# An LSTM step whose unit groups share PSUM columns through zero-padded stationary h, with the RNN beside it in bf16 parts

## The chip, the cores and the metric

The kernel runs on one core of a Trainium2 chip. The metric is the device time of one execution in microseconds, from the first to the last instruction of that core. The kernel before the change takes 4678.84 us (median of 3 runs, 4676.4 to 4680.62).

## The reference

The input is x of 4 x 1024 x 512 (batch B = 4, T = 1024 time steps, width D = 512) and one conditioning vector of 512 per batch row. Four residual layers follow one another, all float32:

```
x = x + rnn(x)        # h = tanh(x_t @ Wx + b + h @ Wh), 1024 steps in a row, Wh 512 x 512
x = x + ssm(x)        # 4-tap conv, projections, state = decay*state + dt*B_t*u_t, output projection
x = x + lstm(x)       # A = x_t @ Wx + b + h @ Wh, Wh 512 x 2048
                      # c = sigmoid(f)*c + sigmoid(i)*tanh(g);  h = sigmoid(o)*tanh(c), 1024 steps in a row
x = x + adapt(x)      # x @ (base + low-rank matrix made from the conditioning vector)
```

The RNN and the LSTM are the recurrences: step t needs the h of step t - 1, and the h of only four batch rows at a time. Everything else can be done for many time steps at once.

## The kernel before, in words

Features lie on the partitions: a vector of 512 is 128 partitions x KC = 4 columns. The time axis is cut into 32 chunks of TC = 32 steps. The main loop (`do_pass`, L815) makes one LSTM step per turn. In the same turn it makes one RNN step, which runs LEAD = 56 steps ahead, and the jobs that a table gives for this place in the chunk: input projections of the RNN (`project0`) and of the LSTM (`input_mm`, L334), the state-space layer (`ssm_jobs`), the last layer (`adapt_mm`, L754). A job stands at "pe" (TensorE, before the RNN's matmuls), "gap" or "end" (VectorE and ScalarE). The order of the instructions on every engine is the order in which this loop writes them; nothing reorders it. Steps before the first LSTM step (the first 56 RNN steps) also load and prepare the weights; these loads are paced by RNN steps (`paced`, L688).

One LSTM step works on h of 128 partitions x 4 columns x 4 batch rows. To get float32 precision from bf16 matmuls, h is split in NP = 3 parts, each the upper 16 bits of what is left (`split`, L208, on VectorE), and Wh in three bf16 parts (`wh2`). In `lstm_mm` (L375 to L388) the 12 columns of a matmul's stationary side are the three parts of h for four batch rows; the moving side is one part of Wh. TensorE is used as four column tiles of 32, one per j, which compute units 128 j to 128 j + 127 and write PSUM partitions 32 j on. The step is cut in two halves of the units, mh = 0 (called A) and mh = 1 (called Bh), with an accumulator `acc2` of 128 x 256 each: 4 gates x 64 units. Per half there are 4 k x 3 parts x 4 tiles = 48 matmuls of 256 columns; kh says which half of h is multiplied, so that A's h of the step before is used first.

Then each half goes through the same chain (class `Half`): VectorE transposes 32 x 32 blocks of `acc2` (L403, gates i, f, g as 128 x 192, gate o as 128 x 64), so that features lie on partitions again; adds the three partial sums and the input part, which ScalarE has copied beside them (L391, L409); ScalarE takes tanh of the gates (L416); VectorE makes products and the cell (L429, L434); ScalarE takes tanh of the cell (L439); VectorE makes h (L442) and splits it twice (L208). A's and Bh's chains are interleaved by hand in `do_pass`.

One RNN step is `rnn_mm` (L349): 4 k x 4 tiles of float32 matmuls with 4 stationary and 128 moving columns, for each of which the profile has two matmul records. Then one transpose of 128 x 128 (L368), one add of the input part (L369), and tanh on ScalarE (L372), which writes h0.

TensorE's order in a turn is: A's matmuls with A's h, a few of Bh's, A's with Bh's h, the rest of Bh's, the "pe" job, the RNN's. GpSimd has nearly nothing to do after the start, where it issues small loads, makes an identity matrix (`make_identity`, L212) and clears buffers.

Of the kernel before, what the change touches and what calls it, by code (L numbers as in the profile page):

```python
# [14 lines left out]
P = 128  # L15
B, T, D = 4, 1024, 512
KC = D // P
TC = 32
# [13 lines left out]
EPS = 1e-5  # L32
XBUFS = 3
# [6 lines left out]
def cond_resid_kernel(ctx: ExitStack, tc: tile.TileContext, a: dict, out: bass.AP):  # L40
# [66 lines left out]
    h2 = [state.tile([P, KC, TC, NP, B], F32, name=f"h2{i}", tag=f"h2{i}") for i in range(2)]  # L107
# [5 lines left out]
    tt2 = [turns(2, f"tt2{m}", [P, 4, 2, B + CT]) for m in range(2)]  # L113
# [3 lines left out]
    tt0 = turns(1, "tt0", [P, KC, CT])  # L117
# [16 lines left out]
    wh0 = load_rows(const, "wh0", a["Wh0"], D, nc.sync)  # L134
# [81 lines left out]
    nc.vector.tensor_scalar(h2[1][:, :, TC - 1, 0, :], condT, 2.0, None, ALU.mult)  # L216
    for n in range(1, NP):
        split(h2[1][:, :, TC - 1], n)
# [6 lines left out]
    acc2 = [psum.tile([P, 2 * P], F32, name=f"acc2{i}", tag=f"acc2{i}") for i in range(2)]  # L225
# [63 lines left out]
    def split_wh2(k, g):  # L289
# [3 lines left out]
        left = xw2[g % 2][:, 2 + g // 2].rearrange("p c t b -> p (c t b)")  # L293
        return (
            lambda: nc.scalar.activation(part[0], upper(w), AF.Copy, scale=scale),
            lambda: nc.vector.scalar_tensor_tensor(left, w, scale, part[0], ALU.mult, ALU.subtract),
            lambda: nc.scalar.copy(part[1], upper(left)),
# [51 lines left out]
    def rnn_mm(c, t):  # L349
        h = h0[c % 2] if t else h0[(c - 1) % 2]  # L350
        for k in range(KC):
            for j in range(4):
                nc.tensor.matmul(  # L353
                    acc0[CT * j : CT * j + B, :],
                    h[:, k, (t - 1) % TC, :], wh0[:, k, j * P : (j + 1) * P],
                    start=(k == 0), stop=(k == KC - 1),
                )
# [7 lines left out]

    def rnn_pre(c, t):
        tt, pre = tt0[0], pre0[t % 2]
        nc.vector.transpose(tt.rearrange("p c b -> p (c b)"), acc0)  # L368
        nc.vector.tensor_add(pre, xw0[c % 2][:, :, t, :], tt[:, :, :B])  # L369

    def rnn_h(c, t):
        nc.scalar.activation(h0[c % 2][:, :, t, :], pre0[t % 2], AF.Tanh)  # L372
# [20 lines left out]
    class Half:  # L393
# [24 lines left out]
        def transpose_o(self):  # L418
            self.transpose(3, 4)
# [559 lines left out]
```

## Time and profile before

| | |
|---|---|
| median of the runs | 4678.84 us |
| span of the profiled execution | 4689.2 us |
| TensorE matmuls, busy | 4552.4 us, 97%, 146,816 instructions |
| TensorE weight loads, busy | 3581.8 us, 146,816 instructions |
| VectorE, busy | 3956.1 us, 84% |
| ScalarE, busy | 1876.6 us, 40% |
| GpSimd, busy | 48.7 us, 1% |
| first LSTM matmul | at 151.3 us |
| one LSTM step | 4.38 us in nearly all steps |

Times are of one profiled execution, in microseconds unless ns is said. In a line of the groups stand the source line, the engine, the operation, output and inputs by name, shapes (partitions x elements), the count, then the busy time and the mean ns of one, and after the bar the idle time of the engine just before such instructions with what ended it. PE is TensorE's matmul, PEld its weight load, DVE VectorE, ACT ScalarE, POOL GpSimd. "issue" is time in which an engine waited for nothing that the profile shows. A line of the DMA queues has packets, MB, and the packets' time as a share of 16 DMA engines over the window. A chain line has start, length and what ran.

### The profile page before, as it was taken

How to read it: one execution, taken by the hardware profiler on the slowest of the kernel's cores; microseconds unless marked ns; L12 is line 12 of the kernel's file. 1: busy time of each engine (PE TensorE's matmuls, PEld its weight loads, DVE VectorE, ACT ScalarE, POOL GpSimd, SP SyncE). 2: the span in 40 equal slices, each digit the busy share in tenths (PEclk: the TensorE clock that was granted, in tenths of full speed). 3: DMA queues.
4: the chain of work that ended last, by engine and by line, in shares of the span. 5: the costliest groups of instructions: out<-in, count | busy, mean ns of one | idle time of the engine just before them, and what ended most of it. 6: DMA issues, size and time to landing. Idle time of an engine off the chain costs nothing.

```text
span 4689.2 us, 326423 instructions
## 1 busy us (share of the span) xinstructions
PE 4552.4 (97%) x146816; PEld 3581.8 (76%) x146816; DVE 3956.1 (84%) x22102; ACT 1876.6 (40%) x9693; POOL 48.7 (1%) x91
## 2 busy tenths in 40 slices
PE   7999999999999999999999999999999999999986
PEld 5777777777877777777777877777777777777754
DVE  4688888888888888888888888888888888888876
ACT  3334444444444444443444444444443444444333
POOL 3000000000000000000000000000000000000000
PEclk9999999999999999999999999999999999999999
DMA  6300000000000000000000000000000000000000
GB/s 155 102 24 7 9 7 9 9 7 9 9 7 9 9 7 9 9 7 9 9 7 9 9 7 9 9 7 9 9 7 9 9 7 9 9 5 7 6 6 8
DMA packets 40234, 67.77 MB, mean 14 GB/s; under 512 B 8864, under 2 KB 26016, under 8 KB 38320
## 3 DMA queue, kind: packets, MB, share of 16 engines
q1 hardware_dynamic: 35792, 46.55, 3.7%
q8 instruction: 1147, 18.79, 1.7%
q14 instruction: 255, 2.09, 0.1%
q0 software_dynamic: 1696, 0.19, 0.0%
q10 hardware_dynamic: 1344, 0.14, 0.0%
HBM read 38.34 MB, written 8.39 MB: 10 GB/s over the span
## 4 chain that ended last, share of the span: by engine, by line
PE 91%; DVE 7%; issue 1%; DMA 0%; POOL 0%; ACT 0%; SPq 0%; DVEq 0%; POOLq 0%
PE acc L384 55%; PE acc L353 18%; PE proj L334 9%; PE pb L308 3%; DVE tt L403 3%; DVE gc L409 2%; PE proj L308 2%; PE ada L754 2%; DVE prod L429 1%; PE ssm_out L308 1%; DVE h L208 1%; PE idle L308 0%; PE pp L616 0%; DVE h L442 0%; DVE tt L368 0%
## 5 line engine op out<-in xcount | busy, mean ns | idle before, releaser
L384 PE MATMUL acc<-wh,h 128*12 128x256 bf16 x98304 | 2908.8, 273 | 96.6 <-DVE h L208 91.0
L384 PEld LDWEIGHTS <-h 128*12 128x12 bf16 x98304 | 2316.3, 87 | 549.0 <-DVE h L208 194.0
L403 DVE STREAM_TRANSPOSE tt<-acc 128x192 f32<-128x192 f32 (+1 forms) x4096 | 1236.6, 310 | 291.0 <-PE acc L384 267.8
L416 ACT ACTIVATE gc<-gc 128x24 f32<-128x24 f32 (+1 forms) x4096 | 854.4, 216 | 1388.5 <-DVE gc L409 1382.9
L353 PEld LDWEIGHTS acc<-wh,h 128*4 128x4 f32 x32768 | 811.6, 87 | 498.9 <-issue 204.2
L353 PE MATMUL acc<-wh,h 128*4 128x128 f32 x32768 | 1089.4, 273 | 12.4 <-ACT h L372 6.6
L409 DVE TENSOR_REDUCE gc<-tt 128x24 f32<-128x96 f32 (+1 forms) x4096 | 1038.9, 255 | 70.5
L208 DVE TENSOR_TENSOR h<-h 128x8 f32<-128x8 f32 (+1 forms) x4098 | 673.2, 164 | 69.9
L372 ACT ACTIVATE h<-pre 128x16 f32<-128x16 f32 x1024 | 221.6, 216 | 1130.9 <-DVE pre L369 1130.9
L439 ACT ACTIVATE th<-gc 128x8 f32<-128x8 f32 x2048 | 427.9, 209 | 261.9 <-DVE gc L434 225.4
L334 PE MATMUL proj<-wx,x 128*32 128x512 f32 x4096 | 530.5, 592 | 0.3 <-issue 0.3
L442 DVE SCALAR_TENSOR_TENSOR h<-gc,th 128x8 f32<-128x8 f32 x2048 | 328.8, 161 | 143.6 <-ACT th L439 133.9
L368 DVE STREAM_TRANSPOSE tt<-acc 128x128 f32<-128x128 f32 x1024 | 316.3, 309 | 68.9 <-PE acc L353 68.8
L429 DVE SCALAR_TENSOR_TENSOR prod<-gc 128x16 f32<-128x16 f32 x2048 | 348.7, 170 | 12.7
L391 ACT COPY tt<-xw 128x32 f32<-128x32 f32 x2048 | 327.9, 207 | 0.0
L434 DVE SCALAR_TENSOR_TENSOR gc<-prod 128x8 f32<-128x8 f32 x2048 | 298.6, 146 | 0.0
L369 DVE TENSOR_TENSOR pre<-xw,tt 128x16 f32<-128x16 f32 x1024 | 180.2, 176 | 37.6
L308 PE MATMUL proj<-xin,wx 128*32 128x128 f32 x4096 | 138.6, 277 | 17.5 <-DMA wh<-in_Wh_dram 11.8
L754 PE MATMUL ada<-layer,x 128*32 128x512 f32 (+1 forms) x1056 | 134.8, 587 | 2.7 <-DVE x L747 2.6
L308 PE MATMUL pb<-x,wp 128*32 128x128 f32 x4096 | 134.7, 273 | 1.0 <-issue 0.6
L308 PEld LDWEIGHTS proj<-xin,wx 128*32 128x32 f32 x4096 | 117.0, 112 | 22.1 <-DMA wh<-in_Wh_dram 11.8
L334 PEld LDWEIGHTS proj<-wx,x 128*32 128x32 f32 x4096 | 119.6, 110 | 5.5 <-issue 0.5
(125 smaller groups left out, 1159.1 us busy)
## 6 DMA issues: line engine op xcount, KB each, us to landing
layer<-in_w2T_dram SPq DMA_DIRECT2D x32, 512.0 KB, 4.6
xin<-in_xT_dram SPq DMA_DIRECT2D x128, 64.0 KB, 2.7
out_dram<-x SPq DMA_DIRECT2D x124, 64.0 KB, 2.1
wx<-in_Wx_dram SPq DMA_DIRECT2D x20, 256.0 KB, 5.1
layer<-in_Wh_dram SPq DMA_DIRECT2D x16, 256.0 KB, 6.0
wh<-in_Wh_dram SPq DMA_DIRECT2D x4, 256.0 KB, 8.3
layer<-in_w_dram SPq DMA_DIRECT2D x4, 256.0 KB, 4.5
layer<-in_base_dram SPq DMA_DIRECT2D x4, 256.0 KB, 8.1
```

What stands on the lines that cost most here:

```text
L208: nc.vector.tensor_tensor(h[:, :, n], h[:, :, n - 1], upper(h[:, :, n - 1]), ALU.subtract)
L308: nc.tensor.matmul(dst[CT * j : CT * (j + 1)], columns(j), x, start=first, stop=final)
L334: nc.tensor.matmul(ps[CT * j : CT * (j + 1), :], tok, w[:, j], start=(k == 0), stop=(k == KC - 1))
L353: nc.tensor.matmul(acc0[CT * j : CT * j + B, :], h[:, k, (t - 1) % TC, :], wh0[:, k, j * P : (j + 1) * P], start=(k == 0), stop=(k == KC - 1),
L384: nc.tensor.matmul(acc2[mh][CT * j : CT * j + NP * B, :], upper(h[:, k, (t - 1) % TC].rearrange("p s b -> p (s b)")), w[:, :, n0 : n0 + 2 ...
L391: nc.scalar.copy(tt2[m][t % 2][:, :, :, :B], xw2[c % 2][:, :, 2 * m : 2 * m + 2, t, :])
L403: nc.vector.transpose(self.tt[:, g0:g1, :, B:].rearrange("p g c b -> p (g c) b"), acc2[self.m][:, 2 * CT * g0 : 2 * CT * g1],)
L409: nc.vector.tensor_reduce(self.gc[:, to : to + g1 - g0].rearrange("p g c b -> p (g c) b"), self.tt[:, g0:g1, :, : (1 + NP) * B].rearrange( ...
L416: nc.scalar.activation(self.gc[:, g0:g1], self.gc[:, g0:g1], AF.Tanh, scale=0.5)
L429: nc.vector.scalar_tensor_tensor(self.prod, self.gc[:, 0:2], 1.0, self.gc[:, 2:4], ALU.add, ALU.mult)
L439: nc.scalar.activation(self.th, self.c, AF.Tanh, scale=0.5)
L442: nc.vector.scalar_tensor_tensor(self.out[:, :, 0], self.gc[:, 4], 1.0, self.th, ALU.add, ALU.mult)
```

## The change

In `lstm_mm` a half's 64 units per tile are cut in two groups of 32, s = 0 and s = 1, which share the same 128 columns of `acc2` (4 gates x 32 units). h's parts are kept as pairs (zeros, h) in a buffer `ring`; a matmul whose stationary columns begin at the zeros has h in the odd blocks of four rows, one that begins four columns later has h in the even blocks. Stationary columns are 24 for s = 1 and 20 for s = 0. So a half takes 96 matmuls of 128 columns and its accumulator is 128 x 128. Each half has one transpose for all gates; the sums of i, f, g and of o stay apart.

`ring` has two halves of KEEP = 4 time steps; in every fourth step GpSimd copies h out of it to `h2` (`keep_h2`) and to `h0` (`keep_h0`), and in every fourth step it clears the half that comes next (`clear`).

From RNN step WHOLE = 50 on, the RNN multiplies three bf16 parts of h (12 stationary columns) with three bf16 parts of Wh0: 48 matmuls of 128 columns per step. VectorE splits the RNN's h in the next turn, between A's transpose and A's sums; a reduce takes the place of the RNN's add, with the input part copied by GpSimd (`rnn_input`). Wh0 is loaded into a buffer of the LSTM's and split during RNN steps 37 to 45 (`split_wh0`). The ring is cleared by GpSimd before the initial h is written.

```diff
...
 NP = 3
 EPS = 1e-5
+WHOLE = LEAD - 6
+KEEP = 4
+LEFT = 5
 XBUFS = 3
...
     x2 = [state.tile([P, KC, TC, B], F32, name=f"x2{i}", tag=f"x2{i}") for i in range(2)]
     xw2 = [state.tile([P, 4, KC, TC, B], F32, name=f"xw2{i}", tag=f"xw2{i}") for i in range(2)]
-    h2 = [state.tile([P, KC, TC, NP, B], F32, name=f"h2{i}", tag=f"h2{i}") for i in range(2)]
+    h2 = [state.tile([P, KC, TC, B], F32, name=f"h2{i}", tag=f"h2{i}") for i in range(2)]
     def turns(n, name, shape):
         return [state.tile(shape, F32, name=f"{name}{i}", tag=f"{name}{i}") for i in range(n)]
-    tt2 = [turns(2, f"tt2{m}", [P, 4, 2, B + CT]) for m in range(2)]
+    ring = turns(2, "ring", [P, KEEP, KC * NP * 3 * B])
+    wide = KC * NP * 2 * B
+
+    def hp2(t):
+        return ring[t // KEEP % 2][:, t % KEEP, :wide].rearrange("p (c s i b) -> p c s i b", c=KC, s=NP, i=2)
+
+    def hp0(t):
+        return ring[t // KEEP % 2][:, t % KEEP, wide:].rearrange("p (c s b) -> p c s b", c=KC, s=NP)
+
+    tt2 = [turns(2, f"tt2{m}", [P, 4, 2 * B + CT]) for m in range(2)]
     gc = [turns(4, f"gc{m}", [P, 5, 2, B]) for m in range(2)]
     prod = [turns(2, f"prod{m}", [P, 2, 2, B]) for m in range(2)]
     th2 = [turns(4, f"th2{m}", [P, 2, B]) for m in range(2)]
-    tt0 = turns(1, "tt0", [P, KC, CT])
+    tt0 = turns(2, "tt0", [P, KC, B + CT])
     pre0 = turns(2, "pre0", [P, KC, B])
     x1 = state.tile([P, KC, 3 + TC, B], F32, name="x1", tag="x1")
...
     load_x(0, a["xT"][0])
     wx0 = load_rows(const, "wx0", a["Wx0"], D, nc.sync)
-    wh0 = load_rows(const, "wh0", a["Wh0"], D, nc.sync)
+    wh0 = xw2[0].rearrange("p g c t b -> p g (c t b)")
+    quads(nc.sync, wh0, a["Wh0"].rearrange("(j c q) n -> j q c n", j=4, c=KC))
+    wh0p = [const.tile([P, KC, D], BF16, name=f"wh0p{i}", tag=f"wh0p{i}") for i in range(NP)]
     prep_ctx = ExitStack()
     prep = prep_ctx.enter_context(tc.tile_pool(name="prep", bufs=1))
...
         nc.vector.memset(h[:, :, TC - 1, :], 0.0)
     nc.vector.tensor_copy(h0[1][:, :, TC - 1, :], condT)
-    nc.vector.tensor_scalar(h2[1][:, :, TC - 1, 0, :], condT, 2.0, None, ALU.mult)
+    for x in ring:
+        nc.gpsimd.memset(x, 0.0)
+    first = hp2(TC - 1)[:, :, :, 1]
+    nc.vector.tensor_scalar(first[:, :, 0], condT, 2.0, None, ALU.mult)
     for n in range(1, NP):
-        split(h2[1][:, :, TC - 1], n)
+        split(first, n)
     for m in range(2):
         nc.vector.memset(gc[m][0][:, 3], 0.0)
...
     nc.vector.memset(s1, 0.0)
     acc0 = psum.tile([P, P], F32, name="acc0", tag="acc0")
-    acc2 = [psum.tile([P, 2 * P], F32, name=f"acc2{i}", tag=f"acc2{i}") for i in range(2)]
+    acc2 = [psum.tile([P, P], F32, name=f"acc2{i}", tag=f"acc2{i}") for i in range(2)]
     for t in (acc0, *acc2):
         nc.vector.memset(t, 0.0)
...
         )
+    def split_wh0(k):
+
+        w, left = wh0[:, k], x2[k % 2].rearrange("p c t b -> p (c t b)")
+        part = [x[:, k] for x in wh0p]
+        return (
+            lambda: nc.scalar.copy(part[0], upper(w)),
+            lambda: nc.vector.tensor_tensor(left, w, part[0], ALU.subtract),
+            lambda: nc.scalar.copy(part[1], upper(left)),
+            lambda: nc.vector.tensor_tensor(part[2], left, part[1], ALU.subtract),
+        )
+
+
     def bank(name, shape, tag="fill", bufs=2):
         return psum.tile(shape, F32, name=name, tag=tag, bufs=bufs)
...
     def rnn_mm(c, t):
-        h = h0[c % 2] if t else h0[(c - 1) % 2]
-        for k in range(KC):
+        if c * TC + t < WHOLE:
+            h = h0[c % 2] if t else h0[(c - 1) % 2]
+            parts = [(h[:, k, (t - 1) % TC, :], wh0[:, k]) for k in range(KC)]
+        else:
+            h = hp0((t - 1) % TC)
+            parts = [
+                (upper(h[:, k].rearrange("p s b -> p (s b)")), w[:, k]) for k in range(KC) for w in wh0p
+            ]
+        for n, (x, w) in enumerate(parts):
             for j in range(4):
                 nc.tensor.matmul(
-                    acc0[CT * j : CT * j + B, :],
-                    h[:, k, (t - 1) % TC, :], wh0[:, k, j * P : (j + 1) * P],
-                    start=(k == 0), stop=(k == KC - 1),
+                    acc0[CT * j : CT * j + x.shape[-1], :], x, w[:, j * P : (j + 1) * P],
+                    start=(n == 0), stop=(n == len(parts) - 1),
                 )
     idle = bank("idle", [P, D], tag="ada", bufs=1)
...
         x = xin[0].rearrange("p c t b -> p (c t b)")
         tiled(idle, lambda j: x[:, :CT], x)
+    def rnn_input(c, t):
+        if c * TC + t >= WHOLE:
+            nc.gpsimd.tensor_copy(tt0[t % 2][:, :, :B], xw0[c % 2][:, :, t, :])
+
     def rnn_pre(c, t):
-        tt, pre = tt0[0], pre0[t % 2]
-        nc.vector.transpose(tt.rearrange("p c b -> p (c b)"), acc0)
-        nc.vector.tensor_add(pre, xw0[c % 2][:, :, t, :], tt[:, :, :B])
+        tt, pre = tt0[t % 2], pre0[t % 2]
+        nc.vector.transpose(tt[:, :, B:], acc0)
+        if c * TC + t < WHOLE:
+            nc.vector.tensor_add(pre, xw0[c % 2][:, :, t, :], tt[:, :, B : 2 * B])
+        else:
+            nc.vector.tensor_reduce(
+                pre, tt[:, :, : (1 + NP) * B].rearrange("p c (s b) -> p c b s", b=B),
+                axis=mybir.AxisListType.X, op=ALU.add,
+            )
     def rnn_h(c, t):
-        nc.scalar.activation(h0[c % 2][:, :, t, :], pre0[t % 2], AF.Tanh)
-
-
-    def lstm_mm(c, t, kh, mh, parts=range(2 * NP)):
-
-
-        h = h2[c % 2] if t else h2[(c - 1) % 2]
-        for x in parts:
-            k, n = 2 * kh + x // NP, x % NP
+        pre, h, parts = pre0[t % 2], h0[c % 2][:, :, t, :], hp0(t)[:, :, 0]
+        if c * TC + t < WHOLE:
+            nc.scalar.activation(h, pre, AF.Tanh)
+        else:
+            nc.scalar.activation(parts, pre, AF.Tanh)
+        if c * TC + t == WHOLE - 1:
+            nc.vector.tensor_copy(parts, h)
+
+    def rnn_split(c, t, n):
+        if c * TC + t >= WHOLE - 1:
+            split(hp0(t), n)
+
+
+    PIECES = [(k, n, s) for k in range(2) for n in range(NP) for s in (1, 0)]
+
+    def lstm_mm(c, t, kh, mh, pieces=slice(0, None)):
+
+
+        h = hp2((t - 1) % TC).rearrange("p c s i b -> p c (s i b)")
+        for k, n, s in PIECES[pieces]:
+            k += 2 * kh
             w = wh2[n][:, k].rearrange("p (g n) -> p g n", g=4)
+            x = upper(h[:, k, B * (1 - s) :])
             for j in range(4):
-                n0 = P * j + 2 * CT * mh
+                n0 = P * j + CT * (2 * mh + s)
                 nc.tensor.matmul(
-                    acc2[mh][CT * j : CT * j + NP * B, :],
-                    upper(h[:, k, (t - 1) % TC].rearrange("p s b -> p (s b)")), w[:, :, n0 : n0 + 2 * CT],
-                    start=(k == 0 and n == 0), stop=(k == KC - 1 and n == NP - 1),
+                    acc2[mh][CT * j : CT * j + x.shape[-1], :], x, w[:, :, n0 : n0 + CT],
+                    start=((k, n, s) == (0, 0, 1)), stop=((k, n, s) == (KC - 1, NP - 1, 0)),
                 )
     def lstm_input(c, t, m):
-        nc.scalar.copy(tt2[m][t % 2][:, :, :, :B], xw2[c % 2][:, :, 2 * m : 2 * m + 2, t, :])
+        nc.scalar.copy(
+            tt2[m][t % 2][:, :, : 2 * B].rearrange("p g (c b) -> p g c b", b=B),
+            xw2[c % 2][:, :, 2 * m : 2 * m + 2, t, :],
+        )
     class Half:
...
             self.m, self.tt, self.gc, self.th = m, tt2[m][t % 2], gc[m][t % 4], th2[m][t % 4]
             self.prod, self.c = prod[m][t % 2], gc[m][(t + 1) % 4][:, 3]
-            self.out = h2[c % 2][:, 2 * m : 2 * m + 2, t]
-
-
-        def transpose(self, g0=0, g1=3):
-            nc.vector.transpose(
-                self.tt[:, g0:g1, :, B:].rearrange("p g c b -> p (g c) b"),
-                acc2[self.m][:, 2 * CT * g0 : 2 * CT * g1],
-            )
+            self.out = hp2(t)[:, 2 * m : 2 * m + 2, :, 1]
+
+
+        def transpose(self):
+            nc.vector.transpose(self.tt[:, :, 2 * B :], acc2[self.m])
         def sum(self, g0=0, g1=3, to=0):
             nc.vector.tensor_reduce(
-                self.gc[:, to : to + g1 - g0].rearrange("p g c b -> p (g c) b"),
-                self.tt[:, g0:g1, :, : (1 + NP) * B].rearrange("p g c (s b) -> p (g c) b s", b=B),
+                self.gc[:, to : to + g1 - g0].rearrange("p g c b -> p g (c b)"),
+                self.tt[:, g0:g1, : 2 * (1 + NP) * B].rearrange("p g (s x) -> p g x s", x=2 * B),
                 axis=mybir.AxisListType.X, op=ALU.add,
             )
         def gates(self, g0=0, g1=3):
             nc.scalar.activation(self.gc[:, g0:g1], self.gc[:, g0:g1], AF.Tanh, scale=0.5)
-
-        def transpose_o(self):
-            self.transpose(3, 4)
         def sum_o(self):
             self.sum(3, 4, to=4)
...
         def split(self, n):
             split(self.out, n)
+
+    def kept(t):
+        return ring[t // KEEP % 2]
+
+    def keep_h2(c, t):
+        if t % KEEP == KEEP - 1:
+            x = kept(t)[:, :, :wide].rearrange("p t (c s i b) -> p c t s i b", c=KC, s=NP, i=2)
+            nc.gpsimd.tensor_copy(h2[c % 2][:, :, t - KEEP + 1 : t + 1, :], x[:, :, :, 0, 1])
+
+    def keep_h0(c, t):
+        if t % KEEP == KEEP - 1 and c * TC + t >= WHOLE:
+            n = min(KEEP, c * TC + t + 1 - WHOLE)
+            x = kept(t)[:, KEEP - n :, wide:].rearrange("p t (c s b) -> p c t s b", c=KC, s=NP)
+            nc.gpsimd.tensor_copy(h0[c % 2][:, :, t - n + 1 : t + 1, :], x[:, :, :, 0])
+
+    def clear(t):
+        if t % KEEP == 1:
+            nc.gpsimd.memset(kept(t + KEEP), 0.0)
...
             if 0 <= n < 4 * KC:
                 at_step(6 + i, stages[n][f])
+
+    for k in range(KC):
+        for n, f in enumerate(split_wh0(k)):
+            at_step(37 + 2 * k + n // 2 + (k // 2), f)
     at_step(17, load_w1)
     for j in range(W2_BUFS):
...
                 A, Bh = Half(c, t, 0), Half(c, t, 1)
                 lstm_mm(c, t, 0, 0)
-                lstm_mm(c, t, 0, 1, (0, 1))
+                lstm_mm(c, t, 0, 1, slice(0, LEFT))
                 lstm_mm(c, t, 1, 0)
-                lstm_mm(c, t, 0, 1, (2, 3, 4, 5))
+                lstm_mm(c, t, 0, 1, slice(LEFT, None))
                 lstm_mm(c, t, 1, 1)
+            before = divmod(c * TC + t + LEAD - 1, TC)
+            if rnn and not lstm:
+                for n in range(1, NP):
+                    rnn_split(*before, n)
             do(t, "pe")
-            if rnn:
+            if rnn and not lstm:
                 rnn_mm(*r)
             if c * TC + t < 8 - TC:
...
             if lstm:
                 A.transpose()
+                if rnn:
+                    rnn_split(*before, 1)
                 A.sum()
-                A.transpose_o()
+                if rnn:
+                    rnn_split(*before, 2)
+                    rnn_mm(*r)
                 A.sum_o()
                 A.gates()
+                A.gate_o()
                 A.products()
-                A.gate_o()
                 Bh.transpose()
                 A.cell()
-                Bh.transpose_o()
                 A.tanh()
                 Bh.sum()
...
                 A.h()
                 Bh.sum_o()
+                Bh.gate_o()
                 A.split(1)
-                Bh.gate_o()
                 Bh.products()
                 A.split(2)
...
                 Bh.split(1)
                 Bh.split(2)
+                keep_h2(c, t)
             if rnn:
+                rnn_input(*r)
                 rnn_pre(*r)
                 rnn_h(*r)
+                keep_h0(*r)
+            if lstm:
+                clear(t)
             do(t, "end")
             while later:
...
```

More of the change, by code (lines that the diff above doesn't have):

```diff
@@ L292, in split_wh2 @@
         part = [x[:, k, cols] for x in wh2]
-        left = xw2[g % 2][:, 2 + g // 2].rearrange("p c t b -> p (c t b)")
+        left = (h2, x2)[g // 2][g % 2].rearrange("p c t b -> p (c t b)")
         return (
@@ L561, in cond_resid_kernel @@
     ae, xc, sq = (prep.tile([P, KC, B], F32, name=x, tag=x) for x in ("ae", "xc", "sq"))
-    ones = xw2[0][:, 0, 0].rearrange("p t b -> p (t b)")
+    ones = xw2[1][:, 3, 0].rearrange("p t b -> p (t b)")
     nc.gpsimd.memset(ones, 1.0 / D)
@@ L747, in adapt_add @@
         nc.vector.scalar_tensor_tensor(
-            x3[:, m, :, t0:t1].rearrange("p b t -> p t b"), h2[c % 2][:, m, t0:t1, 0], 0.5, x2[c % 2][:, m, t0:t1],
+            x3[:, m, :, t0:t1].rearrange("p b t -> p t b"), h2[c % 2][:, m, t0:t1], 0.5, x2[c % 2][:, m, t0:t1],
             ALU.mult, ALU.add,
```

## The prediction

> **What bounds the kernel now.** I read the page first (shares, the chain of waits, the groups), then the groups by shape, the chain in order of time over a few steps, and last, because doubling the matmul count asks for it, the queue that brings TensorE its instructions.
>
> The page: busy shares, the chain, the two matmul groups, the instruction queue.
>
> ```profile
> span 4689.2 us, 326423 instructions
> PE 4552.4 (97%) x146816; PEld 3581.8 (76%) x146816; DVE 3956.1 (84%) x22102; ACT 1876.6 (40%) x9693; POOL 48.7 (1%) x91
> ...
> q8 instruction: 1147, 18.79, 1.7%
> ...
> PE 91%; DVE 7%; issue 1%; DMA 0%; POOL 0%; ACT 0%; SPq 0%; DVEq 0%; POOLq 0%
> ...
> L384 PE MATMUL acc<-wh,h 128*12 128x256 bf16 x98304 | 2908.8, 273 | 96.6 <-DVE h L208 91.0
> L353 PE MATMUL acc<-wh,h 128*4 128x128 f32 x32768 | 1089.4, 273 | 12.4 <-ACT h L372 6.6
> ```
>
> TensorE ends 91% of the chain. One step of the chain (start, length in us) is 2.65 + 0.86 + 0.87 = 4.38 us:
>
> ```profile
> 2404.33 2.65 PE acc L384 x96
> 2406.98 0.86 PE proj L334 x8
> 2407.84 0.87 PE acc L353 x32
> ```
>
> The four column tiles run together, so 96 LSTM matmuls are 24 rounds of 0.110 us, the 32 records of the RNN (two per f32 matmul) 8 rounds of 0.109, and the 8 of 512 columns 2 rounds of 0.430. From the last two, (430-109)/384 = 0.84 ns per f32 column and 2 ns per round; a bf16 column costs half, so a round of 128 bf16 columns streams in 0.056.
>
> The queue line is the one that matters. 18.79 MB in 1147 packets is 16 KB each; 2 x 146,816 = 293,632 PE instructions make it 64 bytes each, so a packet is 256 instructions, 128 matmuls with their weight loads. Here is one such packet, then the chain, then the next packet (40 slices per window; the bytes are drawn where the packet starts):
>
> ```profile
> GB/s 0 0 0 234 0 0 0 0 0 0 0 0 0 0 0 0 0 0 0 0 0 0 0 0 0 0 0 0 0 0 0 0 0 0 0 0 0 0 0 0
> ...
> q8 instruction: 1, 0.02, 2.7%
> ```
>
> ```profile
> 3795.04 2.53 PE acc L384 x95
> 3797.57 0.35 issue
> 3797.92 0.27 PE acc L384
> ```
>
> ```profile
> GB/s 0 0 0 0 0 0 0 0 0 0 0 0 0 0 0 0 0 0 0 0 0 0 0 298 0 0 0 0 0 0 0 0 0 0 0 0 0 0 0 0
> ```
>
> The first window is 3795.0 to 3797.8: the packet starts at 3795.27 and takes 2.7% x 16 x 2.8 = 1.21 us, to 3796.49. TensorE stops one matmul before the end of its 96 with no semaphore to wait for, and goes on at 3797.92, 1.43 us after the landing. The last window is 3797.8 to 3800: the next packet starts in slice 23, at 3799.07, 1.15 us after TensorE went on. I read it so: there is room for two packets; the request for one goes out when the engine enters the other, 1.1 us pass to the transfer, 1.0 to 1.2 in it, 1.4 until it can be used. That is 3.5 us per 256 instructions when TensorE outruns it. Two facts of the trace support this: counting instructions, all 19 stops of over 0.2 us without a wait inside the LSTM's matmuls fall on the same place modulo 256; and no two packets start less than 3.27 us apart (median 4.00), not even where one had come late. A dense stretch now uses 256 instructions in 128 x 27.3 ns = 3.49 us, and a whole step has 256 and the 16 to 64 of a job in 4.38: the fetch just keeps up.
>
> **The change, part by part.**
>
> LSTM matmuls. 96 of 256 columns become 48 pieces x 4 tiles = 192 of 128 columns. Streaming: 24 x 0.110 = 2.65 us becomes 48 x 0.056 = 2.69. Bounds of a round: 0.056 if the weight load (24 or 20 columns instead of 12) stays hidden; about 0.10 if a round cannot be shorter than a weight load, which takes 88 ns for 12 columns and 110 for 32. I take 0.056: after a wait, matmuls start 2 ns after their loads started, so the load's length is latency. PE instructions: 192 become 384 per step.
>
> RNN matmuls. From RNN step 50 on, 16 f32 matmuls (32 records, 64 instructions) become 48 bf16 of 128 columns (96 instructions): 8 x 0.109 = 0.87 us becomes 12 x 0.056 = 0.67.
>
> By streaming alone TensorE's step would be 2.69 + 0.67 + 0.86 + 0.03 of switching = 4.25, against 4.38.
>
> Instruction fetch. Per step 192 + 32 = 224 more: 480, plus 29 on average for the other jobs, is 509, or 1.99 packets. At 3.5 us that is 6.96 us; the streaming of 4.25 lies inside it. Bounds for a packet's period: 3.27 (smallest seen) and 3.8 (the stop shown). I take 3.5, the sum of the usual parts, 1.1 + 1.0 + 1.4.
>
> The Trainium skill, "Runtime: NRT & Kernel Launch", section "Instruction fetch mechanics", also has refills of 16 KiB, 256 instructions, but calls the crossing mostly hidden and gives TensorE 128 KiB; by that the fetch costs nothing and the step is 4.25. The stops shown above, one packet after another without a lead of more than one, speak against it, and I go by them. "TensorE: Matmul & The Clock Gate", section "Wait — 56ns, not 53.3ns?", says starts never come closer than about 25 ns; 240 matmuls would then take 6.0 us and the step 6.9, but here the four tiles of a round start 3 to 4 ns apart.
>
> VectorE. Per half, transposes of 128x192 (0.380) and 128x64 (0.239) become one of 128x128 (0.309 in the RNN's row): -0.62 per step for both. Added: two splits of 128x16 (0.174 each); the RNN's add (0.176) becomes a reduce of 64 to 16 columns, between the 0.205 and 0.305 of the LSTM's, taken at 0.255. Net -0.19. Behind A.transpose, A's chain to its last split shrinks from 2.48 to about 2.26 us and B's from 3.45 to 3.20. All of it runs while TensorE waits for instructions, so I cost it at nothing; without that cover the loop from A.transpose back to itself would be about 4.2, under the 4.25.
>
> New waits. TensorE's RNN matmuls wait for the two RNN splits, which end 0.75 us behind A.transpose; TensorE reaches them after the LSTM's second half and the job, at 0.87 or later: nothing, and LSTM matmuls queued behind are not held.
>
> GpSimd. One copy of 16 columns per step, two of 64 and a memset of 576 per four steps; between the 0.25 of a 1x1 copy and the 0.60 of a 128-column multiply, under 1 us of a step. Beside such a read a VectorE add with two SBUF inputs took 0.29 instead of 0.18, so up to 0.1 for one or two splits in every fourth step. Hidden. ScalarE's work keeps its size and moves by one place.
>
> Start. The initial h now goes to a ring that GpSimd clears first, and VectorE's clearing of acc0, for which the first RNN matmul waits, is queued behind it. GpSimd's DMA issues and mask end at 29.8 us in this trace; two memsets of 576 (0.520 for 512) end at 31.0, and VectorE's 0.9 until acc0 brings the first matmul from 17.7 to about 32. The loads are paced by RNN steps, so +14 us stays. Splitting Wh0 (8 ScalarE copies of 0.61, 8 VectorE subtractions of 0.68) spreads over 9 steps of 2 us with idle time on both: 0 to 10, taken as 2.
>
> The sum. Windows over the trace give 287,929 PE instructions from the first LSTM matmul at 151.3 us on. Add 1024 x 192 and 968 x 32 (the RNN steps from there on): 515,513, or 2014 packets, x 3.5 = 7048. With 151.3 + 14 + 2 ahead and 10 of tail: 7225 as a profiled execution. The profiled 4689.2 lies 10 above the median of 4678.84, so 7215.
>
> **The rivals.**
>
> Faster: the period of 3.5 us is no limit, because a faster engine makes requests earlier. For it: only 39 stops are there, some 18 us in all. Against it: the shortest interval of 3.27, even after late packets. It decides below 4.38 / 1.99 = 2.2 us per packet; then steps of 4.25 give 4679 - 1024 x 0.13 + 16 = 4562.
>
> Weight loads: a round cannot be shorter than its load, 0.10. 60 x 0.10 + 0.86 = 6.9 per step, 4679 + 1024 x 2.5 + 16 = 7255. Same time, another picture: evenly spaced rounds, no stops. Against it: the 2 ns.
>
> Half-way: requests overlap partly and the period is 2.8 us: 2014 x 2.8 + 167 = 5806.
>
> No change at all: matmul gains, start-up and GpSimd cancel. The faster rival with 0.12 us per step given back to GpSimd's lock on VectorE's splits; only if the fetch is no limit.
>
> **How the numbers follow.** Fetch-bound 0.86, weight loads 0.03, half-way 0.05, faster 0.05, no change 0.01. Slower is 0.86 + 0.03 + 0.05 = 0.94. Periods of 3.27 and 3.69 give 6750 and 7600; the fetch case lies in there 9 times in 10, which with the weight loads is 0.8. 0.2% (9 us) is about what can be told from no change here.
>
> **What would show it.** Right: the instruction queue with some 2,040 packets and 33 MB, about 3.5 us apart; TensorE busy in bursts of 256 instructions (1.8 us) with "issue" between them; "issue" leading the chain with over a third; LSTM rounds of 0.056 inside a burst; transposes 128x128 at 0.31; the first RNN matmul near 32 us. Wrong: packets closer than 3 us, or rounds near 0.1 without stops; too small or large if a packet's transfer, 0.9 to 1.4 us here, settles at one end.

## The result, and the profile after

The changed kernel takes 7548.6 us (median of 4 runs, 7536.59 to 7559.6) against 4677.68 for the kernel before: a ratio of 1.6135, 95% interval 1.6112 to 1.6158. The forecast was 7215 us in a range of 6750 to 7600, slower with a chance of 0.94. It was right in sign and cause, and 333 us too low, 51 us inside the upper end of its range.

The page of the changed kernel: the shares, the instruction queue, the chain by engine, and the groups that answer to those shown of before.

```profile
span 7549.7 us, 558534 instructions
PE 4872.8 (65%) x260704; PEld 4045.2 (54%) x260704; DVE 3923.0 (52%) x22011; ACT 1860.7 (25%) x9701; POOL 481.3 (6%) x1823
...
q8 instruction: 2042, 33.46, 1.8%
...
PE 63%; issue 34%; DVE 3%; ACT 0%; DMA 0%; POOL 0%; DVEq 0%; POOLq 0%
...
L442 PE MATMUL acc<-wh,ring 128*24 128x128 bf16 (+1 forms) x196608 | 3299.2, 221 | 2139.4 <-issue 2059.9
...
L463 DVE STREAM_TRANSPOSE tt<-acc 128x128 f32<-128x128 f32 x2048 | 649.2, 317 | 2776.7 <-PE acc L442 2776.2
...
L389 PE MATMUL acc<-wh0p,ring 128*12 128x128 bf16 x46752 | 962.5, 222 | 353.3 <-issue 339.6
```

TensorE was busy for 97% of the span before and is busy for 65% now, and the engine that sits idle is the one that has the work: "issue" (waiting for nothing that the profile shows) is 34% of the chain, where it was 1%. VectorE now waits 2776 us for LSTM matmuls, so its shorter transposes (317 ns where there were 380 and 239) end sooner in a place where nobody needs them. The queue has 2042 packets of 16 KB, 78% more than 1147.

TensorE over 9 us (start, length, what, count, and in brackets the idle time before with what ended it):

```profile
2399.92 1.56 PE L442 MATMUL acc<-wh,ring 128*24 128x128 bf16 x97 [1.61 <-issue]
2401.26 1.07 PE L830 MATMUL ada<-layer,x 128*32 128x512 f32 x8
2402.12 0.51 PE L389 MATMUL acc<-wh0p,ring 128*12 128x128 bf16 x23
2403.67 0.56 PE L389 MATMUL acc<-wh0p,ring 128*12 128x128 bf16 x25 [1.04 <-issue]
2404.01 1.62 PE L442 MATMUL acc<-wh,ring 128*24 128x128 bf16 x103
2407.42 1.46 PE L442 MATMUL acc<-wh,ring 128*24 128x128 bf16 x89 [1.79 <-issue]
```

Between two stops lie 97 + 8 + 23 = 128 matmuls and 25 + 103 = 128 matmuls: with their weight loads 256 instructions, one packet. Where they stop has nothing to do with the program: once inside the RNN's matmuls, once inside the LSTM's.

The instruction queue in the window 2400 to 2407.5 (40 slices of 0.19 us):

```profile
GB/s 0 0 0 0 0 87 0 0 0 0 0 0 0 0 0 0 0 0 0 0 0 0 0 0 0 87 0 0 0 0 0 0 44 0 0 0 0 0 0 0
...
q8 instruction: 2, 0.03, 2.2%
```

The packets start in slices 5 and 25, at 2400.98 and 2404.74. The first lands at 2402.24; TensorE goes on at 2403.67, 1.43 us later, and 1.07 us after that the next packet starts. That is the three-part loop that the prediction read from two packets of before, now in nearly every packet: the 2020 packets from the first LSTM matmul on (167.9 us) start 3.651 us apart on average, and 167.9 + 2020 x 3.651 = 7543.

### The profile page after: what moved, and what is told of

It is laid out like the page before. It is cut to its first block, busy times and chain, and to the rows that moved or that the text cites. A ratio compares the mean times of both kernels' runs of the same rounds, so it can differ in the third digit from the quotient of the medians.

```text
span 7549.7 us, 558534 instructions
## 1 busy us (share of the span) xinstructions
PE 4872.8 (65%) x260704; PEld 4045.2 (54%) x260704; DVE 3923.0 (52%) x22011; ACT 1860.7 (25%) x9701; POOL 481.3 (6%) x1823
## 3 DMA queue, kind: packets, MB, share of 16 engines
q8 instruction: 2042, 33.46, 1.8%
## 4 chain that ended last, share of the span: by engine, by line
PE 63%; issue 34%; DVE 3%; ACT 0%; DMA 0%; POOL 0%; DVEq 0%; POOLq 0%
PE acc L442 41%; PE acc L389 10%; PE proj L363 6%; PE pb L337 2%; PE proj L337 2%; PE ada L830 1%; DVE gc L466 1%; DVE tt L463 1%; PE ssm_out L337 0%; DVE ring L222 0%; DVE ring L496 0%; PE idle L337 0%; DVE prod L483 0%; DVE tt L407 0%; PE pp L688 0%
## 5 line engine op out<-in xcount | busy, mean ns | idle before, releaser
L442 PE MATMUL acc<-wh,ring 128*24 128x128 bf16 (+1 forms) x196608 | 3299.2, 221 | 2139.4 <-issue 2059.9
L442 PEld LDWEIGHTS <-ring 128*20 128x20 bf16 (+1 forms) x196608 | 2889.7, 93 | 2437.0 <-issue 2311.1
L463 DVE STREAM_TRANSPOSE tt<-acc 128x128 f32<-128x128 f32 x2048 | 649.2, 317 | 2776.7 <-PE acc L442 2776.2
L389 PEld LDWEIGHTS <-ring 128*12 128x12 bf16 x46752 | 811.8, 89 | 793.0 <-issue 705.1
L389 PE MATMUL acc<-wh0p,ring 128*12 128x128 bf16 x46752 | 962.5, 222 | 353.3 <-issue 339.6
L222 DVE TENSOR_TENSOR ring<-ring 128x8 f32<-128x8 f32 (+1 forms) x6046 | 965.7, 160 | 70.7 <-ACT ring L421 0.6
L421 ACT ACTIVATE ring<-pre 128x16 f32<-128x16 f32 x974 | 210.3, 216 | 1576.7 <-DVE pre L411 1576.7
L407 DVE STREAM_TRANSPOSE tt<-acc 128x128 f32<-128x128 f32 x1024 | 320.5, 313 | 350.6 <-PE acc L389 350.2
L496 DVE SCALAR_TENSOR_TENSOR ring<-gc,th 128x8 f32<-128x8 f32 x2048 | 342.7, 167 | 144.2 <-ACT th L493 134.0
L411 DVE TENSOR_REDUCE pre<-tt 128x16 f32<-128x64 f32 x974 | 260.0, 267 | 102.9 <-DVE tt L407 2.7
L403 POOL COPY tt<-xw 128x16 f32<-128x16 f32 x974 | 186.1, 206 | 84.6 <-DVE pre L411 70.3
```

Source lines behind the costliest of these rows:

```text
L222: nc.vector.tensor_tensor(h[:, :, n], h[:, :, n - 1], upper(h[:, :, n - 1]), ALU.subtract)
L389: nc.tensor.matmul(acc0[CT * j : CT * j + x.shape[-1], :], x, w[:, j * P : (j + 1) * P], start=(n == 0), stop=(n == len(parts) - 1),)
L442: nc.tensor.matmul(acc2[mh][CT * j : CT * j + x.shape[-1], :], x, w[:, :, n0 : n0 + CT], start=((k, n, s) == (0, 0, 1)), stop=((k, n, s) = ...
L463: nc.vector.transpose(self.tt[:, :, 2 * B :], acc2[self.m])
L496: nc.vector.scalar_tensor_tensor(self.out[:, :, 0], self.gc[:, 4], 1.0, self.th, ALU.add, ALU.mult)
```

## The experiments

Two questions. Is the time really set by the count of TensorE's instructions, and not by their streaming or their weight loads? And what is the rest of the change, the single transposes and the RNN in bf16, worth where the fetch does not cover it? Ratios are to the kernel before on the same chip, with 95% intervals.

**1. The LSTM part alone.** From the changed kernel; the RNN's bf16 parts and the splitting of Wh0 are left out.

```diff
...
-WHOLE = LEAD - 6
+WHOLE = T
...
```

> The changed LSTM alone: the RNN stays in float32, 64 instructions of TensorE per step in the place of 96. Instruction fetch: 968 x 32 / 256 = 121 packets fewer, x 3.65 us (the mean interval of the changed kernel's profile) = -442, so about 7107 us (7050 to 7160), although TensorE gets 0.2 us more to stream in every step. Streaming: the RNN's 12 rounds of 0.056 become 8 of 0.109, +0.2 x 968 = +194, about 7743. Weight loads (a round no shorter than 0.10): 12 x 0.10 become 8 x 0.109, -0.33 x 968 = -319, about 7230, with evenly spaced rounds.

Measured: 7210.3 us, ratio 1.5401 (1.5378 to 1.5424). TensorE has 0.2 us per step more to stream and the kernel is 338 us faster: it has 126 packets fewer. The streaming rival (7743) is out. The weight-load rival's 7230 lies close, but its picture does not: rounds take 0.056 us between the stops. The fetch estimate is 100 us low, and outside its range, because on this chip a packet takes longer: 1894 packets from 162.0 us on, 3.725 us apart; their transfers take 1.12 us on average, 1.065 in the changed kernel's profile. 162 + 1894 x 3.725 = 7217.

**2. Half the moving columns, the same instructions.**

```diff
-                    acc2[mh][CT * j : CT * j + x.shape[-1], :], x, w[:, :, n0 : n0 + CT],
+                    acc2[mh][CT * j : CT * j + x.shape[-1], : 2 * CT], x, w[:, :2, n0 : n0 + CT],
```

> The changed kernel with 64 moving columns instead of 128 in every LSTM matmul, so gates g and o are not multiplied: the same count of instructions, half the streaming. Instruction fetch: no change, 7549 us within 50, rounds inside a burst half as long and the stops longer by the same. Streaming: 48 rounds are 0.028 us shorter, -1.34 x 1024 = -1376, about 6170. Weight loads: no change either, but with no stops.

Measured: 7702.7 us, ratio 1.6442 (1.6415 to 1.647). 1.34 us of streaming less per step bring nothing; the time is even 154 us above the 7549 expected, beyond the 50 allowed. 2020 packets x (3.725 - 3.651) are 149 of them. The same chip as in experiment 1, the same interval of 3.725, and 125 packets more from the first LSTM matmul on: 125 x 3.725 + 9 of a later start = 475 of the 492 us between the two. The page, and two windows of 4 us (window, its length, busy time, granted clock, DMA share, GB/s):

```profile
PE 4663.5 (61%) x260704; PEld 3652.7 (47%) x260704; DVE 3927.3 (51%) x22011; ACT 1855.5 (24%) x9701; POOL 481.0 (6%) x1823
...
q8 instruction: 2042, 33.46, 1.8%
```

```profile
2400.00:2404.00 4.00, 3.43 (x113) 0.50 0.02 4
...
2408.00:2412.00 4.00, 2.41 (x174) 1.00 0.02 4
```

TensorE's clock was granted at 0.803 on average, 0.50 in the first of these windows. Of the whole time 40% has 0.50, and the packets come no later for it: they start 3.72 us apart there and 3.73 us at the full clock.

**3. Instructions alone, added to the kernel before.** Matmuls of 4 columns, 16 of them as shown and, with range(24), 96.

```diff
             do(t, "pe")
+            if rnn and lstm:
+                for n in range(4):
+                    for j in range(4):
+                        nc.tensor.matmul(
+                            acc0[CT * j : CT * j + B, :B], wh2[0][:, 0, :B], wh2[0][:, 0, :B],
+                            start=True, stop=True,
+                        )
             if rnn:
```

> The kernel before with 16 added matmuls of 4 moving columns per step (4 rounds, 32 instructions) in the 968 steps that have an RNN step. Instruction fetch: 287,929 + 968 x 32 = 318,905 instructions from the first LSTM matmul on are 1246 packets, x 3.65 = 4547, and 151 + 10 around them: 4708 us if the room for two packets evens out steps with and without a job; steps with a job have 304 to 352 instructions, 4.3 to 5.0 us, so up to 4890; I take 4780, with more stops than the 39 of before. Streaming: 16 x 4 columns, below 0.02 us a step, at most 4700 and no more stops. A fixed cost of 0.09 to 0.10 us per round (weight loads): +0.36 to 0.40 in every step, 5030 to 5070.

> The kernel before with 96 added matmuls of 4 moving columns per step (24 rounds, 192 instructions). Instruction fetch: 287,929 + 968 x 192 = 473,785 instructions are 1851 packets, x 3.65 = 6756, with 161 around them 6917 us (6800 to 7050), bursts and stops, one packet every 3.65 us. Streaming: 24 rounds of some 0.015 us, +0.36 a step, about 5030. Weight loads: 24 x 0.09 = 2.16 a step, about 6770, with evenly spaced rounds and no stops.

Measured: 4880.95 us with 16, ratio 1.0422 (1.0407 to 1.0438), and 7117.8 us with 96, ratio 1.5199 (1.5168 to 1.5229). The page of the kernel with 96:

```profile
PE 5720.2 (80%) x239744; PEld 4820.5 (68%) x239744; DVE 4061.7 (57%) x22102; ACT 1877.6 (26%) x9693; POOL 48.3 (1%) x91
...
q8 instruction: 1873, 30.69, 1.8%
...
PE 78%; issue 19%; DVE 2%; DMA 0%; POOL 0%; ACT 0%; SPq 0%; DVEq 0%; POOLq 0%
...
L384 PE MATMUL acc<-wh,h 128*12 128x256 bf16 x98304 | 3195.6, 279 | 630.7 <-issue 574.5
```

The old LSTM, untouched, now stops with "issue" for 575 us, and the kernel is 2435 us slower by 192 instructions per step. Undisturbed, the 96 added matmuls take TensorE about 0.8 us of a step, more than the 0.36 expected; by that alone the kernel would take an estimated 4679 + 968 x 0.8 = 5450 us. 1851 packets at the measured 3.757 and 153.6 ahead give 7108. This is the loss of the change without the change. The time lies 200 us above the estimate and outside its range, because the interval is 3.757 and not 3.65. It is also somewhat longer than in experiments 1 and 2 on the same chip, probably because TensorE has data waits here (52 us before the LSTM's matmuls, for VectorE's splits).

With 16 the time lies at the upper end of what was expected of the fetch. Steps of 304 instructions have a median of 4.454 us, 0.07 above the 4.384 of the same steps before, which is the added rounds; their mean is 4.58, and that 0.13 more is stops. The steps with an RNN step have 1.22 packets on average, 4.55 us at this chip's 3.725, and take 4.62: the fetch and TensorE's own work (4.45) bound this kernel nearly alike.

**4. One part of three of Wh, in the changed kernel and in the kernel before.** So few instructions that the fetch leads in neither. The edit in the kernel before; in the changed one the same two lines stand at the head of the loop over the pieces.

```diff
             k, n = 2 * kh + x // NP, x % NP
+            if n:
+                continue
...
```

> The changed kernel with only the first of the three parts of the LSTM's Wh multiplied (the second and third are left out): 128 instructions per step less of the three times 128, so 253,369 from the first LSTM matmul on, 990 packets, x 3.75 = 3710 and about 180 around them, 3890 at least by the fetch. By the chain of waits: B's chain of 3.20 us behind A.transpose, 4 rounds of 0.056 with B's h, some 0.35 of latencies: 3.77 per step, 1024 x 3.77 + 178 = 4040. So the fetch no longer decides alone; I take 4060 (4000 to 4200), below the kernel before cut in the same way by some 150 us. Rival: the shorter transposes are worth nothing even where nothing covers them; then not below that kernel.

> The kernel before with only the first of the three parts of the LSTM's Wh multiplied (the second and third are left out): 64 LSTM instructions per step, 156,857 in all, 613 packets, 2240 us of fetch at most: not the bound. The chain of waits: B's chain of 3.45 us, 2 rounds of 0.110 with B's h, some 0.3 of latencies: 3.96 per step, 1024 x 3.96 + 161 = 4216 (4130 to 4300).

Measured: changed 4350.1 us (ratio 0.9292, 0.9276 to 0.9307), before 4354.2 (0.9304, 0.929 to 0.9318). No difference where 150 us were expected: a miss for both numbers. The chains, changed first:

```profile
DVE 70%; ACT 17%; issue 6%; PE 5%; POOL 1%; DVEq 0%; DMA 0%; ACTq 0%; SPq 0%; POOLq 0%
```

```profile
DVE 84%; PE 7%; issue 4%; ACT 4%; DMA 0%; POOL 0%; SPq 0%; DVEq 0%; POOLq 0%
```

The steps are nearly alike too, 4.07 us on average in the changed kernel and 4.09 in the kernel before; the 20 us by which the changed one's first LSTM matmul comes later (172 against 152) take that back. VectorE's queue sets both. My sum counted a chain of LSTM work; the projections' sums and the RNN's work stand in the same queue. In the changed kernel there is also a new wait, hidden so far by the fetch:

```profile
2403.33 0.27 DVE L411 TENSOR_REDUCE pre<-tt 128x16 f32<-128x64 f32 x1
2403.51 0.31 DVE L465 STREAM_TRANSPOSE tt<-acc 128x128 f32<-128x128 f32 x1
2403.69 0.21 ACT L421 ACTIVATE ring<-pre 128x16 f32<-128x16 f32 x1 [1.29 <-DVE pre L411]
...
2403.93 0.17 DVE L222 TENSOR_TENSOR ring<-ring 128x16 f32<-128x16 f32 x1
2404.03 0.31 DVE L468 TENSOR_REDUCE gc<-tt 128x24 f32<-128x96 f32 x1
```

The RNN's split (L222) is written between A's transpose and A's sums. It waits for the RNN's tanh (L421, which ends at 2403.90), and A's sums wait behind it. The wait itself is small: before its 1950 splits of 128x16 VectorE idles 21.5 us in all, here 0.11 us. Larger is the work that the RNN's part puts into this queue. So the RNN's part might be giving back what the LSTM's part gains.

**5. The same cut without the RNN's part.** Experiments 1 and 4 together: the changed LSTM, one part of Wh, the RNN in float32.

> The changed LSTM with the RNN left in float32, and only the first of the three parts of the LSTM's Wh (the second and third are left out): 128 + 64 + 29 = 221 instructions per step, 0.86 packets, 3.2 us of fetch, so the chain decides. With the RNN's splits the same cut took 4350 us, and the kernel before cut so took 4354 (4.09 a step). If the shorter transposes and chains are worth the 0.19 to 0.2 us a step of the prediction where nothing covers them, and the RNN's two splits on VectorE were what gave it back: 3.90 a step, 1024 x 3.90 + 162 + 10 = 4160 (4090 to 4250). If the LSTM's one transpose lies in waits for ScalarE anyway: 4330 to 4370.

Measured: 4173.9 us, ratio 0.8921 (0.8906 to 0.8936). Once nothing covers it, the changed LSTM (shorter transposes, and the gates in another order) gains what was expected: 3.90 us per step against 4.09. The RNN's part costs 176 us here. VectorE's busy time shows the price, first the changed LSTM alone, then with the RNN's part:

```profile
PE 3140.5 (75%) x114048; PEld 2116.6 (51%) x114048; DVE 3527.7 (85%) x20054; ACT 1761.7 (42%) x9693; POOL 258.8 (6%) x605
```

```profile
PE 3144.0 (72%) x129632; PEld 2114.6 (49%) x129632; DVE 3731.4 (86%) x22011; ACT 1854.7 (43%) x9701; POOL 484.1 (11%) x1823
```

204 us more on VectorE (two splits of 154 ns, and a reduce of 266 for an add of 176, per step; consecutive records overlap, so they add up to more than the busy time grows), and none less on TensorE.

**6. The RNN part alone, on the kernel before.** One tile stands for the three parts of Wh0.

```diff
...
+                if rnn:
+                    rnn_split(*before, 1)
                 A.sum()
+                if rnn:
+                    rnn_split(*before, 2)
+                    rnn_mm(*r)
...
```

> The RNN in bf16 parts alone, in the kernel before, with the changed order of the RNN's splits and matmuls (one tile stands for all three parts of Wh0, so the RNN's weights are not the right ones; counts and sizes are the change's). 32 instructions per step more, as with the 16 added matmuls: 1246 packets. Fetch: that kernel took 4881 with 0.10 a step of streaming that is not here, and TensorE streams 0.2 less: 4720 to 4880, I take 4780. Rival, VectorE: the two splits of 0.174 lie between A's transpose and A's sums, and without the shorter transposes they lengthen A's and B's chains by 0.35: 4.38 becomes 4.73 a step, about 5020, with VectorE a large share of the chain.

Measured: 4908.2 us, ratio 1.0491 (1.0475 to 1.0506). Neither number. The chain over 4.5 us, in order of time (start, length, what), from one step's sums to the next:

```profile
2399.82 0.31 DVE gc L457
2400.13 0.08 DVE ring L218
2400.21 0.17 DVE tt L451
...
2401.99 1.83 PE acc L432 x56
2403.84 0.38 DVE tt L451
2404.23 0.06 DVE ring L218
2404.28 0.31 DVE gc L457
```

A loop of 4.47 us, 1.83 of it TensorE and the rest VectorE: 0.09 above the 4.38 of before, not 0.35, presumably because the splits lie partly in VectorE's waits for ScalarE. That is the median step (4.476 at 304 instructions); the mean step is 4.64, and the 0.16 between is of the kind seen with 16 added matmuls, which have the same count of instructions ("issue" is 4% of this chain). So both causes seem to be at work; some 8 us more are a later first LSTM matmul (159.9 against 151.4). How the 229 us divide exactly stays open, because a stop of the fetch and a wait for VectorE can hide each other.

**7. One transpose per half without doubling the matmuls.** If the change's gain is one transpose for all gates, it could be had with 256 columns. The same was tried with the third part of Wh left out, as in experiment 4, so that TensorE does not bound the step.

```diff
-        def transpose(self, g0=0, g1=3):
+        def transpose(self, g0=0, g1=4):
...
-                A.transpose_o()
...
-                Bh.transpose_o()
```

> The kernel before with one transpose of 128x256 per half in the place of 128x192 and 128x64: the change's one transpose without its matmuls, the instructions of TensorE as before. The 128x256 transpose of the projections took 0.44 us, so 0.06 more ahead of A's sums and 0.24 - 0.06 = 0.18 less behind them per half. TensorE's own work (2.65 + 0.86 + 0.87) stays and bounds the step; its matmuls wait 91 us in all for VectorE's splits. If these waits go: 4590 to 4660. If the later sums cost what the shorter chain gives, or TensorE alone decides: 4670 to 4700. I take 4640.

> The kernel before with two of the three parts of the LSTM's Wh (the third is left out): 64 LSTM matmuls per step, TensorE 1.77 + 0.86 + 0.87 = 3.50 us a step, 209 instructions. If VectorE and its chain bound it as with one part (4.09 a step, VectorE 84% of the chain), 4354 and up to 0.22 us a step more for the 2 rounds with B's h that lie on the loop: 4350 to 4580, I take 4400. If TensorE bounded it: 3.5 x 1024 + 161 = 3750.

> The same two parts of three of the LSTM's Wh, and one transpose of 128x256 per half. VectorE has 2 x 0.18 = 0.36 us less per step. If VectorE and its chain bound the step, 0.18 to 0.36 a step less than with two transposes: 184 to 370 us less, I take 250 less, about 4150. If the transposes are not what counts: as with two transposes.

Measured: 4733.6 us, ratio 1.0116 (1.0101 to 1.0131), for the full kernel. With two parts of Wh: 4468.6 (0.9549, 0.9534 to 0.9563) with two transposes, 4524.3 (0.9667, 0.965 to 0.9683) with one. The single wide transpose costs 52 and 56 us, where it was to save 40 and 250: a miss for both. VectorE in the kernel before, and with one transpose (start, length, what):

```profile
2405.94 0.38 DVE L403 STREAM_TRANSPOSE tt<-acc 128x192 f32<-128x192 f32 x1 [0.50 <-PE acc L384]
2406.36 0.32 DVE L409 TENSOR_REDUCE gc<-tt 128x24 f32<-128x96 f32 x1
2406.60 0.24 DVE L403 STREAM_TRANSPOSE tt<-acc 128x64 f32<-128x64 f32 x1
2406.87 0.22 DVE L409 TENSOR_REDUCE gc<-tt 128x8 f32<-128x32 f32 x1
2407.01 0.17 DVE L429 SCALAR_TENSOR_TENSOR prod<-gc 128x16 f32<-128x16 f32 x1
```

```profile
2405.59 0.45 DVE L403 STREAM_TRANSPOSE tt<-acc 128x256 f32<-128x256 f32 x1
2406.07 0.45 DVE L409 TENSOR_REDUCE gc<-tt 128x24 f32<-128x96 f32 x2
2406.69 0.18 DVE L429 SCALAR_TENSOR_TENSOR prod<-gc 128x16 f32<-128x16 f32 x1 [0.17 <-ACT gc L416]
```

In the kernel before, gate o's transpose and sum run while ScalarE takes the tanh of the other gates. With one transpose VectorE idles 0.17 us there, and the sums that ScalarE waits for come 0.07 later (446 ns against 380). From A's transpose to A's products it is 1.10 us instead of 1.07. With two parts of Wh VectorE is busy for 73 us less with one transpose (3842.0 against 3914.6), and ScalarE's share of the chain grows from 3% to 15%. So leaving out the second transpose does not pay by itself. This points to the first transpose being short as what pays in the change's LSTM part: 317 ns for 128x128 is less than 380 for 128x192. No run varies that alone.

**8. The start.**

```diff
     for x in ring:
-        nc.gpsimd.memset(x, 0.0)
+        nc.vector.memset(x, 0.0)
```

> The changed kernel with the ring cleared by VectorE in place of GpSimd. If the clearing behind GpSimd's DMA issues is what moved the start: first RNN matmul back from 34.45 to about 18.5 us, first LSTM matmul from 167.9 to 152 to 155, the whole time 14 to 16 us less at the same packet interval. If it is the splitting of Wh0 or its load: the first RNN matmul comes early, and the first LSTM matmul stays at 165 to 168. The packet interval of this run also says what the chip of this call gives the changed kernel, 3.65 or 3.72.

Measured: 7541.4 us, ratio 1.6113 (1.6081 to 1.6145), too close to the changed kernel's to tell apart by the medians; by the profiles the span is 7536.4 instead of 7549.7 at an interval of 3.652 instead of 3.651. The first RNN matmul is back at 16.3 us, the first LSTM matmul at 155.3. So 12.6 of the 16.5 us go when GpSimd no longer clears the ring. The remaining 4 are probably Wh0's load and splitting: experiments 1 and 5, which leave GpSimd's clearing as it is and Wh0 as it was before, have their first LSTM matmul at 162.0 and 159.1, 6 to 9 us earlier than the changed kernel. As two kernels with the same start differ by 3 us, how the 16.5 divide is not known better than that.

## Why the prediction was right

**The bound** was named rightly, and shown: instructions with next to no columns cost the time (3), half the columns at the same count of instructions save none (2), and a part with fewer instructions and more work gains (1). The faster rival needed packets less than 2.2 us apart, the half-way one 2.8; in four kernels that the fetch bounds throughout (the changed one, 1, 2 and the 96 added matmuls) the mean interval is 3.65 to 3.76 and the smallest 3.2. The weight-load rival needed rounds of 0.10; they take 0.056 between the stops.

**The term that was mis-sized** is the packet's period, 3.5 us by "the usual parts, 1.1 + 1.0 + 1.4". Counted over some 1970 stops of more than 0.2 us in the changed kernel, the transfer takes 1.065, the time until use 1.382 and from there to the next packet 1.204, in all 3.651. The transfer was too small even by the kernel before, where its 1147 packets take 1.118 on average. Of the 0.10 in the last part half is 1.1 for a median of 1.149; the other half is a tail of longer cases. Behind those, TensorE's next 128 instructions take 1.21 us instead of 0.97, so waits and long projections may be the reason; that was not tested. I had taken typical values where a sum over 2014 packets wants means. 2014 x 0.151 = 304 us of the 325 by which the profiled time was missed (7549.7 against 7225); six packets more than counted are another 21. The rest of the miss of 333 is that the profiled time lay 10 above the median before and at it after.

That 7549 lies within 6750 to 7600 is in part luck. On the chip of experiments 1 to 3 a packet takes 3.725 us, and experiment 2, which has the changed kernel's count of instructions, took 7703 there. The stop that the prediction shows adds up to 3.8; its range ended at 3.69.

**LSTM and RNN rounds**: 0.056 predicted, 0.056 measured. **Chains**: A's last split 2.28 us behind A.transpose (2.26 predicted), B's 3.25 (3.20), in the step at 2400.45, where TensorE does not stop between the halves; in the median step it does, and they are 3.96 and 4.93.

**"Costs nothing"** was right only because of the cover. The prediction's net gain of 0.19 us a step on VectorE holds the RNN's splits and reduce: 0.62 less for the LSTM's transposes, 0.43 more for the RNN. With the fetch out of the way the LSTM's part takes 0.19 off a step (5) and the RNN's puts 0.16 on again, so that 0.03 is left (4). Less work on VectorE was thus not as much less time. That the expectation of experiment 5, which took the net 0.19 for the LSTM's part alone, came true is partly luck. The new wait that I had looked for at TensorE's RNN matmuls is 7.4 us in all, as good as nothing; one that I had not looked for is at A's sums, behind a split that waits for the RNN's tanh, and it is small too.

**Start**: +16 predicted, +16.5 measured. The parts differ a little: the first RNN matmul came at 34.45, not 32, since the 128x16 write of the initial h took 2.12 us on VectorE while GpSimd cleared further buffers. It ended at 33.70, and GpSimd's last clearing at 33.66. In experiment 8, where no clearing by GpSimd runs beside it, the same write takes 0.17 us.

**Room for packets, and the floor of a round.** The Trainium skill, "Runtime: NRT & Kernel Launch", section "Instruction fetch mechanics", calls the crossing of a packet's boundary mostly hidden and gives TensorE 128 KiB, room for eight packets; here each packet costs 3.65 us, a third of which TensorE stands still, and room for two fits the stops, so the measurement decides. A note in the same section has the store as only two lines of 16 KiB, which agrees. "TensorE: Matmul & The Clock Gate", section "Wait — 56ns, not 53.3ns?", has a floor of about 25 ns between starts. Most of the added rounds of 4 columns start 25 to 34 ns apart, so here the floor fits a round of four column tiles and not each matmul of it; the 6.0 us that the prediction worked out by that rule counted matmuls.

## What to carry to other kernels

Count TensorE's instructions per step as a resource with a rate of its own: here 256 of them, 128 matmuls with their weight loads, in about 3.65 us, so a step of 4.38 us has room for some 300. Splitting a matmul into narrower ones that stream the same can cost nothing in the engine's own time and 60% of the kernel; look at the instruction queue's packets and at "issue" stops inside a run of matmuls before doing so. And a second instruction that ran while another engine was awaited cost nothing here; merging it into the first lengthened the part that was awaited.

## What the runs showed of the hardware that I had not expected

- The packet's period differs between chips: 3.725 us on the one that ran experiments 1 to 3, 3.65 on the one of experiment 8, with transfers of 1.11 to 1.12 and 1.06 us. Why the chips differ, no run shows. The kernel before, which the fetch does not bound, shows nothing of this (4683 and 4679 us).
- With 64 columns TensorE was granted 0.803 of its clock, against 0.984 for the changed kernel, though both run the same count of instructions from the same 2042 packets. The Trainium skill, "TensorE: Matmul & The Clock Gate", section "Part 1: The HAM clock gate", has half the clock where recent activity is low, and the 0.50 agrees. It cost no time: the interval is the 3.725 of experiment 1, which had a clock of 0.983 on the same chip. TensorE's speed did not count in this kernel, which the fetch bounds.
- A transpose's time grows with its width: 128x256 took 446 ns, 128x192 380, 128x128 317 and 128x64 239, about 69 ns per 64 columns on a fixed 170.
